# Dilated attention and a binary convolution on one core: from which chunk on the order of the instruction queues is written out by hand

## The chip, the core and the metric

The kernel runs on one core of one Trainium2 chip. The metric is device time in microseconds (us), the median of several executions; for the kernel before these were 5062.21, 5062.40 and 5062.62 us. A core has five engines, each with its own instruction queue that is worked off in order: TensorE (PE, matrix products), VectorE (DVE), ScalarE (ACT), GpSimd (POOL) and SyncE (SP, which here only issues DMAs). An instruction that waits for another engine holds up everything behind it in its own queue. So the order of the five queues, fixed when the program is built, is part of the kernel.

## The reference

Input `x` is 16 images of 56 x 56 pixels with 384 channels, float32. Two layers follow each other:

```python
# layer 0: dilated local attention, on the group-normalised input
x = x + _L0_conv_ref(_gn(x), L0_conv_w_qkv, L0_conv_w_proj, L0_conv_b_proj)
# layer 1: depthwise 3x3 convolution with weights clipped and reduced to their sign
x = x + _L1_conv_ref(_gn(x), L1_conv_w)

# in _L0_conv_ref: three channel groups with dilations 1, 2 and 3, four heads of 32 channels each
qkv = jnp.einsum('bchw,oc->bohw', xc, w_qkv)
attn = jnp.einsum('bgdn,bgdkn->bgnk', qg, ku) * scale     # 9 neighbours of each pixel
attn = jax.nn.softmax(attn, axis=-1)
out = jnp.einsum('bgnk,bgdkn->bgnd', attn, vu)
return jnp.einsum('bhwc,oc->bhwo', y, w_proj) + b_proj
```

`_gn` normalises over 32 groups of 12 channels, with mean and variance over a whole image. So nothing of an image can be normalised before all of it has been read.

## The kernel before

**Chunks and three plans.** An image is cut into 7 chunks of 8 rows (448 pixels), which makes 112 chunks. Three plans work on a chunk:

- `plan_a` (L453) reads it (`xin`, L469), turns pixels into columns on PE (`pt_x`, L474: three groups of four transposes), copies the result out of PSUM on ACT (L487), takes statistics on DVE (L489) and stores it in DRAM as `xd` (L492, L494). Of image 0 the turned chunks also stay on chip as `x_first`; chunks 10, 12 and 14 read into a second kind of buffer (`xin_z`), since `xin` has one buffer only.
- `plan_b` (L508) is the attention: load `xn` (L518), normalise (ACT, L522), project k and v (`pkv`, L526; copied to halo buffers by ACT, L539; halo rows passed between neighbouring chunks by small DMAs, L547 and L548), project q (`pq`, L526). DVE multiplies q by the shifted k (`t`, L591, nine instructions of three neighbours each), PE sums over a head's channels in three bursts of 8, 8 and 11 (`ps`, L572), then comes the softmax (L611 to L646; it ends with a DMA that writes `aT`). PE spreads the weights (`pb_a`, L658, nine times), DVE multiplies them by the shifted v (`w`, L669), POOL adds up (L679 to L683), PE applies the output projection (`po`, L696), DVE adds residual and bias (L701).
- `plan_c` (L733) is the convolution of the second layer. It starts ten chunks after `plan_b`, so it plays no part in the first ten chunks. The mean and scale that it needs in another layout go through a small DRAM tile (`mrd` and `mrz`, L404 to L412).

**Order by due times.** Every step is a "piece" with a due time. The table `WHEN` (L34 to L65) gives the due times of the steps of one chunk in units of which 9 (`STEP`, L949) make a chunk; `put` (L426) adds the chunk's start. Chunk m of `plan_b` starts at 9 m, its first steps are due at negative offsets. Everything that prepares the constants and reads image 0 is due before 0. At the end the pieces are traced in the order of their due times (L1007).

**Who decides the order of a queue.** Left alone, the framework's scheduler places instructions when the program is built: it goes by priority, which follows the order of tracing, but lets an instruction pass others that by its own reckoning cannot start yet. `pin` (L986) takes this freedom away: it gives each new instruction a dependence, without a semaphore, on the instruction traced before it on the same engine, so the queue is exactly the traced one. It does so for pieces whose due time lies between `FROM` and `UNTIL` (L952, L1008). Before the change this holds from due time 0 on, on all five engines.

**Bursts.** `in_one_go` (L335) keeps a group of matmuls together. In a pinned piece they simply follow each other; in a piece that is not pinned the first is placed like any other instruction, and the rest get high priority and keep their order.

Of the kernel before, what the change touches and what calls it, by code (L numbers as in the profile page):

```python
# [70 lines left out]
def dilated_attention_then_binary_conv(  # L71
# [33 lines left out]
    N = B * NCH  # L105
# [316 lines left out]
    def at(when, piece):  # L422

        pieces.setdefault(round(when, 4), []).append(piece)
# [524 lines left out]
    STEP = 9  # L949
    FIRST = -200  # L950
    FIXED = [getattr(mybir.EngineType, name) for name in FIXED_ENGINES]
    FROM, UNTIL = 0, STEP * N + 14  # L952
    at(FIRST + .14, load_weights)
    for cc in range(NG):
        at(FIRST + 6 + 2 * cc + .12, lambda cc=cc: turn_qkv_weights(cc))
# [84 lines left out]
```

## Time and profile before

| | |
|---|---|
| median of 3 runs | 5062.4 us |
| the profiled execution | 5064.99 us |
| its span, first to last instruction | 5063.3 us |
| PE busy | 4883.1 us, 96% of the span |
| DVE busy | 4455.8 us, 88% |
| POOL busy | 4224.4 us, 83% |
| ACT busy | 2524.2 us, 50% |
| granted PE clock, mean | 0.98 |
| chain that ended last | PE 86%, DVE 4%, DMA 4% |

The page divides the span into 40 slices and gives for each the tenths of it that an engine was busy; other views give the busy time of every engine in stretches that one chooses, and the instructions of a stretch in order of time. In these, a bracket at the end of a line gives how long the engine had been idle before it and what ended that. The clock granted to PE is given as a share of full speed.

### The profile page before, as it was taken

Reading aid. Unit: us, or ns where it says so; the run is one execution under the profiler, and the core shown is the slowest. Engines: PE = TensorE matmul, PEld = TensorE weight load, DVE = VectorE, ACT = ScalarE, POOL = GpSimd, SP = SyncE. Lnnn points to the kernel's source line nnn. Section 1 sums busy time; section 2 is a strip of 40 time slices with the busy share of each in tenths; the row PEclk is TensorE's granted clock in tenths of the full one; section 3 lists DMA queues with packets and bytes.
Section 4 is the critical chain, followed back from the end, with each engine's and each line's share of the span. In section 5 each row is a group of like instructions: output and inputs, shape, how many; then the busy total and the mean of one; then the engine's idle time right before and its main releaser. Section 6 shows DMA issues by size and latency. Waiting matters only on the chain.

```text
span 5063.3 us, 70210 instructions
## 1 busy us (share of the span) xinstructions
PE 4883.1 (96%) x24325; PEld 2249.2 (44%) x24325; DVE 4455.8 (88%) x4559; ACT 2524.2 (50%) x4501; POOL 4224.4 (83%) x2862
## 2 busy tenths in 40 slices
PE   7899999999999999999999999999999999999965
PEld 4444444444444444444444444444444444444422
DVE  4788999999999999999999999999999999888856
ACT  3122555555555555555555555555555555555445
POOL 2577889888898888889888888888889888898970
PEclk9999999999999999999999999999999999999976
DMA  5344666666666666666666666666666666655545
GB/s 155 108 126 118 176 176 172 174 169 176 168 183 172 170 173 170 176 175 182 165 178 176 177 177 176 180 173 172 178 163 182 176 169 174 156 147 141 141 135 153
DMA packets 831098, 836.43 MB, mean 165 GB/s; under 512 B 379796, under 2 KB 800023, under 8 KB 830743
## 3 DMA queue, kind: packets, MB, share of 16 engines
q1 hardware_dynamic: 822758, 819.95, 61.5%
q10 hardware_dynamic: 7984, 12.00, 0.7%
q8 instruction: 192, 3.15, 0.3%
q14 instruction: 164, 1.34, 0.1%
HBM read 477.52 MB, written 231.24 MB: 140 GB/s over the span
## 4 chain that ended last, share of the span: by engine, by line
PE 86%; DVE 4%; DMA 4%; POOL 2%; ACT 2%; SPq 2%; issue 1%; ACTq 0%; DVEq 0%; POOLq 0%
PE pkv L526 27%; PE pq L526 15%; PE po L696 14%; PE ps L572 11%; PE pc L817 6%; PE pb_a L658 5%; PE pt_x L474 3%; PE pt_o L908 3%; DVE t L591 2%; DMA xd<-xa 1%; DVE w L669 1%; PE pt_s L615 1%; ACT z L786 1%; POOL w L679 1%; DMA mrz<-mrd 0%
## 5 line engine op out<-in xcount | busy, mean ns | idle before, releaser
L679 POOL TENSOR_TENSOR w<-w 128x1344 f32<-128x1344 f32 x672 | 2054.6, 3057 | 275.3 <-DVE w L669 268.4
L669 DVE TENSOR_TENSOR w<-pb_a,v 128x1344 f32<-128x1344 f32 x1008 | 1561.4, 1549 | 231.6 <-PE pb_a L658 164.2
L591 DVE TENSOR_TENSOR t<-pq,k 128x1344 f32<-128x1344 f32 x1008 | 1542.2, 1549 | 100.6 <-PE pq L526 98.8
L526 PE MATMUL pkv<-xn,wqkvT 128*128 128x448 f32 x3924 | 1593.0, 547 | 0.0
L526 PEld LDWEIGHTS pkv<-xn,wqkvT 128*128 128x128 f32 x3924 | 718.5, 190 | 644.6 <-issue 623.2
L696 PE MATMUL po<-y,wprojT 128*128 128x448 f32 x2016 | 808.3, 546 | 8.8 <-POOL y L683 8.8
L526 PE MATMUL pq<-xn,wqkvT 128*128 128x448 f32 x1962 | 807.5, 548 | 7.9 <-DVE t L591 7.8
L572 PE MATMUL ps<-t,sel 128*32 128x448 f32 x6048 | 659.0, 545 | 9.4 <-DVE t L591 9.4
L891 POOL TENSOR_TENSOR m<-m 128x1344 f32<-128x1344 f32 x210 | 639.6, 3046 | 27.3 <-ACT m L881 19.1
L786 ACT ACTIVATE z<-z,mrz 96x448 f32<-96x448 f32 x840 | 570.3, 753 | 29.2 <-DMA mrz<-mrd 24.2
L881 ACT ACTIVATE m<-zg,ktap 128x448 f32<-128x448 f32 x945 | 540.7, 658 | 3.6 <-POOL m L891 3.6
L696 PEld LDWEIGHTS po<-y,wprojT 128*128 128x128 f32 x2016 | 378.5, 193 | 351.1 <-issue 320.3
L611 ACT COPY sT<-ps 128x448 f32<-128x448 f32 x112 | 59.8, 534 | 894.8 <-PE ps L572 894.8
L526 PEld LDWEIGHTS pq<-xn,wqkvT 128*128 128x128 f32 x1962 | 354.4, 190 | 312.7 <-issue 300.4
L539 ACT COPY k<-pkv 128x448 f32<-128x448 f32 x336 | 180.9, 538 | 575.4 <-PE pkv L526 574.9
L683 POOL TENSOR_TENSOR y<-y,w 128x448 f32<-128x448 f32 x336 | 382.7, 1139 | 26.3
L682 POOL TENSOR_TENSOR y<-w 128x448 f32<-128x448 f32 x336 | 382.4, 1138 | 26.3
L658 PE MATMUL pb_a<-aT,spread 24*128 24x448 bf16 x3024 | 368.9, 359 | 23.9 <-DVE w L669 22.6
L817 PE MATMUL pc<-z,kdiag 96*32 96x440 f32 x3360 | 360.6, 548 | 28.6 <-ACT z L749 18.8
L658 PEld LDWEIGHTS <-spread 24*128 24x128 bf16 x3024 | 99.8, 91 | 648.7 <-issue 567.1
L914 ACT COPY osb<-pt_o 112x384 f32<-112x384 f32 x420 | 199.1, 474 | 291.9 <-PE pt_o L908 284.3
L636 POOL TENSOR_TENSOR rest<-ew,e 112x512 f32<-112x512 f32 x112 | 129.9, 1159 | 240.1 <-ACT e L633 240.1
(136 smaller groups left out, 4817.6 us busy)
## 6 DMA issues: line engine op xcount, KB each, us to landing
z<-x1d SPq DMA_DIRECT2D x570, 224.0 KB, 4.3
xr<-xd SPq DMA_DIRECT2D x112, 672.0 KB, 4.9
x1d<-xr SPq DMA_DIRECT2D x112, 672.0 KB, 3.5
xn<-xd SPq DMA_DIRECT2D x109, 672.0 KB, 4.8
xin<-in_x_dram SPq DMA_DIRECT2D x105, 672.0 KB, 7.3
xd<-xa SPq DMA_DIRECT2D x315, 224.0 KB, 4.3
out_dram<-osb SPq DMA_DIRECT2D x420, 168.0 KB, 4.1
x<-x1d SPq DMA_DIRECT2D x80, 560.0 KB, 5.2
```

What stands on the lines that cost most here:

```text
L526: nc.tensor.matmul(dst[:, :PX], wqkvT[:, cc, o0 : o0 + P], had["xn"][:, cc, :], start=(cc == 0), stop=(cc == NG - 1))
L572: return nc.tensor.matmul(had["ps"][32 * j : 32 * j + 32, :PX], sel[:, s0 : s0 + 32], tk, start=(issued[j] == 1), stop=(issued[j] == len(r ...
L591: nc.vector.tensor_tensor(t.rearrange("p k (r w) -> p k r w", w=W), q3, k3, ALU.mult)
L658: return nc.tensor.matmul(pb[:, kx, :PX].rearrange("p (s n) -> p s n", s=NSUB), spread[rows_of, v % 2, :], had["a"][rows_of, :, v // 8, :] ...
L669: nc.vector.tensor_tensor(w.rearrange("p k (r w) -> p k r w", w=W), pb[:, :, :PX].rearrange("p k (r w) -> p k r w", w=W), three(kv[1][g][m ...
L679: nc.gpsimd.tensor_tensor(w0, w0, w, ALU.add)
L683: nc.gpsimd.tensor_tensor(y, y, w0[:, 2], ALU.add)
L696: nc.tensor.matmul(po[:, :PX], wprojT[:, g, j * P : (j + 1) * P], had[f"y{g}"], start=(g == 0), stop=(g == NG - 1))
L786: nc.scalar.activation(z, z, AF.Identity, bias=mrz[:, j, q, 0:1], scale=mrz[:, j, q, 1:2])
L817: return nc.tensor.matmul(pcr[q * HD : (q + 1) * HD, :, x0:x1], kdiag[:, kx // 2, j * NQ + q, :], rows(set_of(j, q))[:, :, x0 + kx - 1 : x ...
L881: nc.scalar.activation(rows(t[:, kx]), zp[:, ky : ky + ROWS, kx : kx + W], AF.Copy, scale=ktap[:, JG, o : o + 1])
L891: nc.gpsimd.tensor_tensor(had["m"], had["m"], t, ALU.add)
```

## The change

One line: the lower bound of the range in which pieces are pinned.

```diff
@@ -949,7 +949,7 @@
     STEP = 9
     FIRST = -200
     FIXED = [getattr(mybir.EngineType, name) for name in FIXED_ENGINES]
-    FROM, UNTIL = 0, STEP * N + 14
+    FROM, UNTIL = 9 * STEP, STEP * N + 14
     at(FIRST + .14, load_weights)
```

Pieces due from 0 up to 81, which are those of the first nine chunks, are no longer pinned; they join those due before 0, which were not pinned either. From 81 on nothing changes: the first pinned instruction of each engine hangs on the last one traced before it. No instruction is added or removed, no buffer changes its size. The passage of mean and scale through DRAM is in both kernels and untouched.

Instructions per engine and where the two built programs differ in order:

| engine | instructions | first place that differs | last place that differs |
|---|---|---|---|
| PE | 18287 | 151 | 1132 |
| DVE | 4561 | 8 | 301 |
| ACT | 4542 | 46 | 185 |
| POOL | 2867 | 93 | 262 |
| SP | 3461 | 21 | 172 |

The last differing PE place falls at about 390 us in the trace of the kernel before.

## The prediction

> **What bounds the kernel now.** I read the page's slices first, then the busy time in stretches of 100 us.
>
> ```profile
> PE   7899999999999999999999999999999999999965
> PEclk9999999999999999999999999999999999999976
> ...
> 0.00:100.00 100.00, 65.48 (x289) 43.14 (x292) 36.39 (x67) 29.51 (x55) 24.89 (x136) 0.92 0.56 159
> 100.00:200.00 100.00, 84.08 (x374) 38.67 (x368) 71.42 (x68) 22.39 (x43) 42.26 (x23) 0.94 0.42 117
> 200.00:300.00 100.00, 97.66 (x434) 45.09 (x433) 85.58 (x88) 22.00 (x41) 72.34 (x56) 0.98 0.42 119
> 900.00:1000.00 100.00, 100.00 (x495) 46.92 (x489) 92.30 (x93) 49.97 (x89) 89.23 (x60) 1.00 0.61 155
> ```
>
> The third number of a stretch is PE's busy time, the clock stands third from the end. From 500 us on PE has hardly a gap: what is gained before that moves the whole rest forward, and nothing else can gain. The change reorders only up to about 390 us. So the question is how much PE time is lost there, and how much of it the new order wins back.
>
> PE's instructions in order of time, those with idle time ahead of them:
>
> ```profile
> 65.05 2.52 PE L526 MATMUL pkv<-x_first,wqkvT 128*128 128x448 f32 x6 [1.13 <-ACT x_first L522]
> 68.06 0.57 PE L474 MATMUL pt_x<-ident,xin 112*128 112x112 f32 x4 [0.49 <-DMA xin<-in_x_dram]
> 77.83 2.49 PE L526 MATMUL pq<-x_first,wqkvT 128*128 128x448 f32 x6 [1.65 <-DVE t L591]
> 97.59 4.15 PE L572 MATMUL ps<-t,sel 128*32 128x448 f32 x22 [4.58 <-DVE t L591]
> 112.34 0.57 PE L474 MATMUL pt_x<-ident,xin_z 112*128 112x112 f32 x4 [2.74 <-DMA xin_z<-in_x_dram]
> 128.71 1.71 PE L572 MATMUL ps<-t,sel 128*32 128x448 f32 x16 [0.36 <-DVE t L591]
> 137.75 3.81 PE L572 MATMUL ps<-t,sel 128*32 128x448 f32 x22 [4.28 <-DVE t L591]
> 154.38 0.57 PE L474 MATMUL pt_x<-ident,xin_z 112*128 112x112 f32 x4 [3.74 <-DMA xin_z<-in_x_dram]
> 198.28 0.98 PE L474 MATMUL pt_x<-ident,xin_z 112*128 112x112 f32 x4 [3.89 <-DMA xin_z<-in_x_dram]
> ```
>
> With four more between 168 and 222 us (0.81, 0.23, 0.81, 0.15) that is 24.9 us of idle time between 60 and 240 us. From 240 to 390 us only 0.86 us per chunk of 39.6 us are left (0.30 before a `pb_a`, 0.56 elsewhere). Two causes stand out: the first transposes of chunks 10, 12 and 14 wait for their load, and the third score burst waits for the last products `t`.
>
> A gap costs more than its length. The clock around the gap that ends at 97.59:
>
> ```profile
> 94.00:96.00 2.00, 0.00 (x0) 0.00 (x0) 2.00 (x3) 0.00 (x0) 0.00 (x0) 1.00 0.00 0
> 96.00:98.00 2.00, 0.41 (x4) 0.17 (x8) 1.54 (x2) 0.00 (x0) 0.00 (x0) 0.94 0.00 0
> 98.00:100.00 2.00, 2.00 (x16) 0.64 (x11) 0.00 (x0) 0.00 (x0) 0.00 (x0) 0.50 0.00 0
> 100.00:102.00 2.00, 2.00 (x11) 0.50 (x5) 0.00 (x0) 0.18 (x1) 0.00 (x0) 0.71 0.00 0
> 102.00:104.00 2.00, 2.00 (x6) 0.90 (x5) 0.00 (x0) 0.35 (x1) 0.00 (x0) 1.00 0.00 0
> ```
>
> Half clock from 97.7 to 101.2 us, 3.4 us long. The burst of 22 rows took 4.15 us; at the 1.71 us of 16 rows it would be 2.35, so 1.8 us are lost. In such stretches half clock also stands at 138.7 (3.4 us), 155.8 (3.4) and 196.7 (6.8, of which PE worked 5.3). Lost: 1.7 + 1.7 + 1.7 + 2.6 = 7.7 us. [...] In all 24.9 + 7.7 = 32.6 us are lost between 60 and 240 us.
>
> [...] gaps of 3.74 to 4.58 us brought half clock, in multiples of 3.41 us, the one of 2.74 us did not. [...]
>
> ```profile
> 83.74 0.54 SPq L469 DMA_DIRECT2D xin<-in_x_dram  x1
> 105.23 0.34 SPq L492 DMA_DIRECT2D xd<-xa  x1
> ...
> 106.84 0.58 SPq L469 DMA_DIRECT2D xin_z<-in_x_dram  x1
> ```
>
> For 21 us SP issued nothing: a store stood waiting for its copy on ACT, with the load of chunk 10 three places behind. Issued at 106.84, it let PE start at 112.34.
>
> **The change part by part.** I compared the built orders and gave each instruction its duration from this trace; times below are on the clock of before.
>
> *Loads of chunks 10, 12 and 14.* In the new SP queue the loads into `xin_z` for 10 and 12 stand before every store of `xa` and every halo copy; each waits only for the transposes of image 0 that free its buffer (done by 36 and 40 us). That of chunk 14 stands ahead of the halo copies of v of its turn and long after chunk 10's transposes. So all three land tens of us early. The gain is 2.74 + 3.74 + 3.89 = 10.4 us of idle time and 1.7 + 2.6 = 4.3 us of clock: 14.7 us.
>
> *Third burst of chunk 0.* Before, PE goes from `pq` straight to the burst of 11 and waits for three `t` (4.49 us). Now three `pkv` (2.4 us) and four transposes (0.57 us) stand between. 4.58 - 3.0 leaves 1.6; I take 1.8[...]. Gain 2.8 + 1.7 = 4.5 us. In chunk 1 three `pkv`, four transposes and two `pb_a` stand there; with DVE's `w` between the `t` I find 2.0 us left in two pieces: 2.3 + 1.7 = 4.0 us.
>
> *First chunks.* ACT now normalises chunks 0 and 1 in one go while PE is still on the first k, so the 1.13 us at 65.05 go; `pkv` for chunk 1 now stands before the second `pq`, so the 1.65 us at 77.83 go; of the 0.49 at 68.06 (a load issued at the same moment as before) 0.2 go. Together 3.0 us. The rest (0.36 + 0.81 + 1.19 = 2.4 us) I leave.
>
> Sum: 14.7 + 4.5 + 4.0 + 3.0 = 26.2 us.
>
> *What it costs at the front.* DVE prepares the small weights (L291 to L319) before the last seven statistics of image 0, where it used to do so from 64 us on; they wait for the nine small loads of L258. The last of these was issued at 29.94 and its kind lands in a median of 4.5 us: 34.4. Twenty instructions take 3.5 us (64.26 to 67.73 before), to 37.9; seven statistics of 0.63 to 42.3, an aggregate 0.34, two statistics 1.26, two aggregates 0.53: 44.4, where before the last ended at 43.55. All that PE can do next hangs on it: 0.9 us lost. If a small load lands at its slowest 10.8 us it would be up to 7 us, my outer bound[...].
>
> *Softmax on POOL.* In the new order the second `w` sum of a pair goes ahead of the softmax remainder, and two `y` sums of 1.14 us stand among its parts. A steady chunk before:
>
> ```profile
> 325.56 1.16 POOL L636 TENSOR_TENSOR rest<-ew,e 112x512 f32<-112x512 f32 x1 [6.32 <-ACT e L633]
> 328.66 2.92 SPq L644 DMA_TRANSPOSE aT<-e  x1
> 336.61 0.37 PE L658 MATMUL pb_a<-aT,spread 24*128 24x448 bf16 x3
> ```
>
> The `w` sum (3.06 us) fits into the 6.32 us that POOL stood idle. The two `y` put `aT` off by 2.3 us. It lands 4.1 us after its issue, at 332.8; the first `pb_a` of the chunk came at 336.61, so 3.8 us are to spare. Hidden by 1.5 us; without that cover each us of delay is a us of PE per chunk.
>
> *Waits not foreseen.* Going through a steady chunk in the new order, I found PE waiting nowhere over 0.1 us, with DVE 4 us short of full. The first chunks are less regular. Bounds: -4 us (the 0.86 us of four steady chunks vanish) to +12 (2 us in each of six). I take +3.
>
> Net: 26.2 - 0.9 - 3 = 22.3, so 22 us. On the profiled execution: span 5063.3 - 22 = 5041.3, with the 1.7 us around it 5043. The profiled run is 2.6 us above the median of the runs, so the median becomes 5062.4 - 22 = 5040.4.
>
> **The rivals.**
>
> *The waits only move.* PE ahead of its feeders finds DVE or ACT late instead: the 14.7 us of the loads are won, but the bursts lose as much elsewhere and the front costs 2 to 7 us. Net 3 to 13 us, middle 8: 5054. For it: DVE is 82% busy at 180 to 200 us (16.35 of 20), and ACT now has three normalisations of `xn` ahead of the copy of the scores. Against: a DVE 71% busy between 100 and 200 us has room.
>
> *Slower: `aT` comes too late in every chunk.* If the remainder on POOL waits not for two `y` but for a backlog of `w`, `aT` is late by 5 us beyond its cover in the seven chunks 2 to 8. [...] 7 x 6.7 = 47 us against 25 won, 5084. It decides from 3.6 us per chunk on (7 x 3.6 = 25). Against: POOL is 72% busy there and was idle just before the remainder.
>
> *It does nothing.* The built orders differ in some 900 places on PE alone; excluded.
>
> **How the numbers follow.** Forecast 0.70 (gains of 14 to 32 us), waits only move 0.20 (0.08 of it still over 0.2%), slower 0.10 (0.08 by over 0.2%). A measurement of this kernel tells about 0.2%, 10 us, from no change. Faster 0.70 + 0.08 = 0.78; same 0.12 + 0.02 = 0.14; slower 0.08. The range: the forecast's best, 32 us, gives 5030; upwards it takes in most of the second case, 5056. Left out are the slower case and a little of the rest, some 0.15.
>
> **What would show it.** Right: no wait of PE for `xin_z` below 250 us; full clock from about 60 us on; no gap over 3.4 us; the first `pb_a` near 115 us instead of 122.98; PE over 93 us busy between 100 and 200 us. The first normalisation on ACT, 52.64 before, at about 53.5 (front cost). Wrong: PE waiting for `aT` or `w` in every chunk from 200 to 390 us, half clock in the slices after the first, or gaps that open after 390 us in the part whose order is unchanged.

## The result, and the profile after

| | before | changed |
|---|---|---|
| median | 5062.0 us (6 runs) | 5044.4 us (6 runs) |
| profiled execution | 5064.99 us | 5046.37 us |
| its span | 5063.3 us | 5044.6 us |

The ratio is 0.9967, with a 95% interval of 0.9957 to 0.9977: 17.6 us faster by the medians, where 22 were forecast. That is a third of a percent, and clear of the noise. On a second chip, beside the experiments below, the same kernel again gave 0.9967 (0.9956 to 0.9978).

The page of the changed kernel, the same two rows as before:

```profile
PE   7999999999999999999999999999999999999965
PEclk8999999999999999999999999999999999999975
```

And its busy time in stretches of 100 us (PE busy is the third number, the clock stands third from the end):

```profile
100.00:200.00 100.00, 96.08 (x448) 43.83 (x447) 87.61 (x85) 26.43 (x49) 58.81 (x33) 1.00 0.46 126
200.00:300.00 100.00, 94.01 (x420) 42.01 (x413) 79.66 (x79) 19.33 (x34) 67.47 (x56) 0.97 0.34 101
300.00:400.00 100.00, 98.49 (x427) 44.14 (x427) 89.72 (x86) 21.70 (x40) 70.53 (x43) 1.00 0.38 106
```

Between 100 and 200 us PE works 96.1 us instead of 84.1, as hoped. Between 200 and 300 us it works 94.0 where it worked 97.7 before: something was lost there that the prediction did not have. PE's waits in the changed kernel, in order of time, show what:

```profile
69.35 0.57 PE L474 MATMUL pt_x<-ident,xin 112*128 112x112 f32 x4 [0.67 <-DMA xin<-in_x_dram]
95.63 4.15 PE L572 MATMUL ps<-t,sel 128*32 128x448 f32 x22 [1.94 <-DVE t L591]
130.01 2.46 PE L572 MATMUL ps<-t,sel 128*32 128x448 f32 x22 [1.44 <-DVE t L591]
145.48 2.52 PE L526 MATMUL pq<-x_first,wqkvT 128*128 128x448 f32 x6 [0.18 <-DVE t L591]
155.57 0.37 PE L658 MATMUL pb_a<-aT,spread 24*128 24x448 bf16 x3 [1.88 <-DVE w L669]
198.72 1.71 PE L572 MATMUL ps<-t,sel 128*32 128x448 f32 x16 [0.41 <-DVE t L591]
219.89 0.35 PE L377 MATMUL pv<-dev,gsel 128*32 128x1 f32 x6 [1.06 <-POOL dev L372]
229.37 1.43 PE L397 MATMUL pp<-pair,gselT 32*128 32x2 f32 x6 [4.67 <-POOL pair L392]
```

The waits for `xin_z` are gone and the two long waits before the third bursts are 1.9 and 1.4 us. New are two waits for POOL in the statistics of image 1 (`group_norm`, L345), the second followed by half clock from 229.18 to 236.01 us:

```profile
229.18:236.01 6.83, 6.64 (x16) 4.04 (x16) 3.63 (x4) 0.39 (x1) 0.28 (x2) 0.50 0.59 160
```

The lead of the changed kernel, as the start of the first `pb_a` of a chunk before less that after, in the two profiled executions:

| first `pb_a` of chunk | 0 | 1 | 2 | 3 | 4 | 5 | 6 | 7 |
|---|---|---|---|---|---|---|---|---|
| before, us | 123.0 | 168.5 | 216.0 | 257.5 | 297.0 | 336.6 | 376.2 | 415.8 |
| lead, us | 7.5 | 12.9 | 23.1 | 13.0 | 13.8 | 14.6 | 15.4 | 16.0 |

23 us are won by chunk 2, 10 are lost before chunk 3, 0.8 us a chunk come back. From there on the lead keeps between 15.8 and 18.9 us.

Why POOL was late, in its own order of time:

```profile
221.57 0.18 POOL L388 TENSOR_TENSOR var<-var 32x1 f32<-32x1 f32 x1 [1.73 <-DVE var L385]
...
222.89 0.18 POOL L389 TENSOR_TENSOR var<-var 32x1 f32<-32x1 f32 x1
223.04 1.15 POOL L636 TENSOR_TENSOR rest<-ew,e 112x512 f32<-112x512 f32 x1
224.17 0.18 POOL L390 TENSOR_SCALAR var<-var 32x1 f32<-32x1 f32 x1
224.43 0.18 POOL L391 TENSOR_TENSOR var<-var 32x1 f32<-32x1 f32 x1
224.56 0.60 POOL L640 CAST e<-rest 112x512 bf16<-112x512 f32 x1
225.14 0.18 POOL L388 TENSOR_TENSOR var<-var 32x1 f32<-32x1 f32 x1
225.28 1.12 POOL L682 TENSOR_TENSOR y<-w 128x448 f32<-128x448 f32 x1
...
229.13 0.18 POOL L392 TENSOR_TENSOR pair<-pair 32x1 f32<-32x1 f32 x1
```

The thirteen small operations of L388 to L392 each use the result of the one before. In the free order, sums of `y` and parts of the softmax stand between them. The thirteen took 7.74 us (221.57 to 229.31); in the kernel before they stood together and took 3.36 us (241.61 to 244.97), from first to last:

```profile
241.61 0.18 POOL L388 TENSOR_TENSOR var<-var 32x1 f32<-32x1 f32 x1 [1.67 <-DVE var L385]
...
244.79 0.18 POOL L392 TENSOR_TENSOR pair<-pair 32x1 f32<-32x1 f32 x1
```

### The profile page after: what moved, and what is told of

Read it like the earlier page. It is cut to its first block, busy times and chain, and to the rows that moved or that the text cites. A ratio compares the mean times of both kernels' runs of the same rounds, so it can differ in the third digit from the quotient of the medians.

```text
span 5044.6 us, 70251 instructions
## 1 busy us (share of the span) xinstructions
PE 4881.7 (97%) x24325; PEld 2246.1 (45%) x24325; DVE 4453.8 (88%) x4559; ACT 2525.3 (50%) x4501; POOL 4223.8 (84%) x2862
## 4 chain that ended last, share of the span: by engine, by line
PE 82%; DMA 3%; DVE 3%; POOL 2%; ACT 1%; SPq 1%; issue 1%; ACTq 0%; DVEq 0%; POOLq 0%
PE pkv L526 26%; PE pq L526 14%; PE po L696 13%; PE ps L572 11%; PE pc L817 7%; PE pb_a L658 5%; PE pt_o L908 3%; PE pt_x L474 2%; DMA xd<-xa 1%; DVE t L591 1%; PE pt_s L615 1%; ACT z L786 1%; DVE w L669 1%; POOL w L679 1%; DMA mrz<-mrd 0%
## 5 line engine op out<-in xcount | busy, mean ns | idle before, releaser
L682 POOL TENSOR_TENSOR y<-w 128x448 f32<-128x448 f32 x336 | 382.3, 1138 | 25.7
L658 PE MATMUL pb_a<-aT,spread 24*128 24x448 bf16 x3024 | 368.9, 359 | 22.8 <-DVE w L669 22.4
L572 PEld LDWEIGHTS ps<-t,sel 128*32 128x32 f32 x6048 | 179.7, 109 | 322.1 <-issue 293.9
```

What stands on the lines that cost most here:

```text
L572: return nc.tensor.matmul(had["ps"][32 * j : 32 * j + 32, :PX], sel[:, s0 : s0 + 32], tk, start=(issued[j] == 1), stop=(issued[j] == len(r ...
L658: return nc.tensor.matmul(pb[:, kx, :PX].rearrange("p (s n) -> p s n", s=NSUB), spread[rows_of, v % 2, :], had["a"][rows_of, :, v // 8, :] ...
```

## Experiments

Each run was timed in five rounds beside the kernel before on the same chip; the two groups were on a second chip, where the kernel before took 5055.3 us (25 runs) and 5055.4 us (26 runs). The only trace of before is from the first chip, so all leads are counted against that one. The changed kernel itself has leads of 26.9, 18.4 and 21.4 us at chunks 2, 3 and 7 on the second chip, 3.7 to 5.4 us more than on the first. So a lead of a run on the second chip is read against these numbers, or against the same trace's lead at another chunk. By their intervals the gains in time are good to 3 to 7 us.

### Is the loss at 220 to 236 us the fault of the order, or does a lead have to fall back there?

**Pinned from chunk 4 on.** The statistics of image 1 are due from 38.5 to 47.

```diff
-    FROM, UNTIL = 9 * STEP, STEP * N + 14
+    FROM, UNTIL = 4 * STEP, STEP * N + 14
```

> Pinned from due time 36 on (chunk 4) instead of 81, so that the statistics of image 1 (due 38.5 to 47) are in the written order again. Theory 1 (the new order won about 23 us by 193 us, and lost 9 of them because the statistics of image 1 were torn apart on POOL): no PE wait for POOL before pp near 230 us, no half clock there, first pb_a of chunk 3 about 22 us ahead of the kernel before, time 8 us under the changed kernel, about 5036. Theory 2 (PE had simply run ahead of what DVE and POOL can feed, so the lead has to fall back at that point whatever the order): a lead of 13 to 16 us again at 260 us, time within 2 us of the changed kernel, 5044.

Measured: 5032.8 us, ratio 0.9952 (0.9940 to 0.9965), 22.4 us under the kernel before and 5.4 under the changed kernel on that chip, where 8 were expected. No wait of PE for POOL stands in its trace between 51 us and the end phase, and no half clock between 55 us and the end phase. The lead is 24.9 us at chunk 2 and still 24.9 at chunk 7. The 0.30 and 0.56 us per chunk of the written order are back:

```profile
263.86 0.36 PE L658 MATMUL pb_a<-aT,spread 24*128 24x448 bf16 x3 [0.30 <-DVE w L669]
265.33 2.52 PE L526 MATMUL pq<-xn,wqkvT 128*128 128x448 f32 x6 [0.56 <-DVE t L591]
```

A lead need not fall back; theory 2 falls by the trace, since the times of the two kernels overlap in their intervals.

**POOL alone in the written order for the small operations.**

```diff
-            pin(FIXED if newest["pinned"] else ())
+            pin(FIXED if newest["pinned"] else FIXED[3:4] if 44.6 <= when < 45.6 else ())
```

> The changed kernel, with POOL alone pinned for the pieces due from 44.6 to 45.6: the thirteen small operations of the statistics of image 1 stand together again ahead of the softmax remainder, all else stays free. Theory 1: the thirteen take 3.4 us instead of 7.7, the 4.67 us wait before pp falls to under 1.5, no half clock at 229 us (another 3.4), so 6 to 8 us under the changed kernel, about 5037. Theory 2 (the lead falls back whatever the order): within 2 us of the changed kernel.

Measured: 5034.4 us, ratio 0.9955 (0.9941 to 0.9968), 20.9 us under the kernel before, against 17.2 for the changed kernel on that chip. POOL and PE in its trace:

```profile
217.64 0.18 POOL L388 TENSOR_TENSOR var<-var 32x1 f32<-32x1 f32 x1 [2.70 <-DVE var L385]
...
220.81 0.18 POOL L392 TENSOR_TENSOR pair<-pair 32x1 f32<-32x1 f32 x1
```

```profile
221.05 0.83 PE L397 MATMUL pp<-pair,gselT 32*128 32x2 f32 x6 [0.28 <-POOL pair L392]
234.93 0.36 PE L658 MATMUL pb_a<-aT,spread 24*128 24x448 bf16 x3 [1.98 <-DMA aT<-e]
```

The thirteen take 3.35 us, the wait before `pp` falls from 4.67 to 0.28 us, and there is no half clock. Part is given back: the softmax that now stands behind them and between two sums of `w` has its `aT` late, and PE waits 1.98 us for it. From chunk 2 to chunk 3 the lead falls by 3.4 us, where it falls by 8.5 in the changed kernel on that chip. So the traces show the small operations on POOL as the cause of the long wait and of the half clock behind it. In time the gain is nearer 4 us than the 6 to 8 expected, and single runs of the two kernels mix (5027.8 to 5035.8 us against 5033.6 to 5045.8), so the time by itself does not show it.

**Free, pinned at the statistics, free again.**

```diff
-        newest["pinned"] = FROM <= when < UNTIL
+        newest["pinned"] = 4 * STEP <= when < 48 or FROM <= when < UNTIL
```

> The changed kernel, with everything pinned once more for due times 36 to 48 alone, where the statistics of image 1 are worked out; free again from 48 to 81. Theory 1: the loss at the statistics goes (6 to 9 us), and the waits of 0.3 and 0.56 us per chunk that the written order has in chunks 5 to 8 stay away as they do in the changed kernel, 0.8 us per chunk: 2 to 3 us better than pinned from 36 on, so 24 to 27 us under the kernel before. Theory 2 (a lead has to fall back at that point): as the changed kernel.

Measured: 5031.9 us, ratio 0.9952 (0.9938 to 0.9965), 23.5 us under the kernel before, where 24 to 27 were expected. The lead is 24.3 us at chunk 3 and 26.5 at chunk 7. The loss is gone and the 2 us of the steady chunks show in the trace; in the times the two are not to be told apart (0.9952 both).

### What carries the 23 us: the early loads or PE's order?

**Only SP's queue free** (from the kernel before; the other four built orders are identical to it).

```diff
-            pin(FIXED if newest["pinned"] else ())
+            pin(() if not newest["pinned"] else FIXED[:4] if when < 9 * STEP else FIXED)
```

> The kernel before, with SP's queue alone left free below due time 81; the four other queues are exactly as before. Theory 1 (loads won 14.7 us by themselves): no PE wait for xin_z, the waits of 4.58 and 4.28 us before the third bursts stay with their half clock, time 14 to 15 us under the kernel before, about 5048. Rival (the gain is that of PE's order, and early loads only move the wait to the next operand): under 6 us, above 5056.

Measured: 5050.9 us, ratio 0.9988 (0.9982 to 0.9995; 21 runs): 4.4 us. PE's waits:

```profile
98.13 3.82 PE L572 MATMUL ps<-t,sel 128*32 128x448 f32 x22 [4.58 <-DVE t L591]
115.42 2.52 PE L526 MATMUL pq<-x_first,wqkvT 128*128 128x448 f32 x6 [2.19 <-DVE t L591]
...
137.47 4.63 PE L572 MATMUL ps<-t,sel 128*32 128x448 f32 x22 [4.28 <-DVE t L591]
156.31 0.37 PE L658 MATMUL pb_a<-aT,spread 24*128 24x448 bf16 x3 [2.19 <-DVE w L669]
157.77 2.52 PE L526 MATMUL pq<-x_first,wqkvT 128*128 128x448 f32 x6 [0.57 <-DVE t L591]
```

No wait for `xin_z` is left, but at each of the three places PE now runs a few us further and waits for DVE: 2.19; 2.19 and 0.57; and 0.57 and 0.56 near 199 us. Of 10.4 us of idle time, 6.1 have only moved. The 4.3 that are left are close to the 4.4 measured, but this sum leaves the clock out: from 60 to 240 us half clock stands for 10.2 us here and for 17.1 before, and the lead in this trace is 7.6 us from chunk 2 on. The traced run, 5047.4 us, was 3.5 us under the median. The forecast of theory 1, 14 to 15 us for the loads by themselves, is refuted; the rival's "under 6 us" came out.

**All but SP's queue free** (from the changed kernel).

```diff
-            pin(FIXED if newest["pinned"] else ())
+            pin(FIXED if newest["pinned"] else FIXED[4:] if when >= 0 else ())
```

> The changed kernel, with SP's queue pinned from due time 0 as in the kernel before; the other four queues are free below 81. Theory 1: the waits for xin_z are back (10.4 us and half clock, 14.7 together), the bursts and first chunks keep their 11.5 us, the statistics still lose 9: about 3 us under the kernel before, 5057 to 5062. Rival (PE's order carries the gain): 10 us or more under the kernel before.

This edit also pins SP after `UNTIL`, which was not meant; from the start of the last output projection to the end its trace takes 150.3 us, and the ten traces lie between 149.5 and 153.8, so nothing shows of it. Measured: 5041.8 us, ratio 0.9968 (0.9955 to 0.9980), 13.4 us under the kernel before. Only one wait for `xin_z` came back (3.33 us at 179 us). SP issues the three loads at 93.65, 129.76 and 173.72 us instead of 106.84, 148.86 and 192.65: the store ahead of the first waits for its copy on ACT, which now starts at 91.48 us instead of 104.67. Free orders elsewhere bring that copy forward; PE's alone brings it to 97.85, in a trace shown below, and which of the others does the rest was not taken apart. Theory 1's 5057 to 5062 is refuted; the rival's "10 us or more" came out.

**Only PE's queue free, and PE's and SP's.**

```diff
-            pin(FIXED if newest["pinned"] else ())
+            pin(FIXED if newest["pinned"] else FIXED[1:] if 0 <= when < FROM else ())
```

> The kernel before with PE's queue alone left free below due time 81; DVE, ACT, POOL and SP are exactly as before. Theory 3 (what counts is that PE has something to do while it waits; early loads only shift a wait): 10 to 18 us under the kernel before, more than the loads alone won, first pb_a of chunk 1 over 8 us ahead, and no loss at the statistics of image 1, since POOL is in the written order. Theory 1 (loads 14.7, bursts and first chunks 11.5, separately): 7 to 11 us, and the waits for xin_z of 2.7 to 3.9 us stay.

For the second, `FIXED[1:4]` takes the place of `FIXED[1:]`, with this expected:

> PE's and SP's queues free below due time 81; DVE, ACT and POOL exactly as before. Theory 3: 2 to 5 us better than PE alone, at or above the changed kernel's gain, 16 to 22 us under the kernel before. Theory 1: the sum of 14.7 and 7 to 11, so 22 to 26 us. If the orders of DVE and ACT were needed for the gain: no better than PE alone.

Measured: PE alone 5044.8 us, ratio 0.9981 (0.9974 to 0.9987; 21 runs), 10.6 us; PE and SP 5029.7 us, 0.9950 (0.9937 to 0.9962), 25.7 us. PE's waits with PE alone free, first, and with both, second (the waits from 52 us to 430 us that are over 2 us, and in the second the one before them):

```profile
105.31 0.98 PE L474 MATMUL pt_x<-ident,xin_z 112*128 112x112 f32 x4 [3.24 <-DMA xin_z<-in_x_dram]
134.29 3.63 PE L572 MATMUL ps<-t,sel 128*32 128x448 f32 x22 [2.20 <-DVE t L591]
149.22 0.98 PE L474 MATMUL pt_x<-ident,xin_z 112*128 112x112 f32 x4 [4.65 <-DMA xin_z<-in_x_dram]
192.49 0.57 PE L474 MATMUL pt_x<-ident,xin_z 112*128 112x112 f32 x4 [3.79 <-DMA xin_z<-in_x_dram]
```

```profile
94.36 2.46 PE L572 MATMUL ps<-t,sel 128*32 128x448 f32 x22 [1.94 <-DVE t L591]
127.96 2.46 PE L572 MATMUL ps<-t,sel 128*32 128x448 f32 x22 [2.19 <-DVE t L591]
```

With PE alone the long waits before the bursts shrink to 1.94 and 2.20 us, and the loads are waited for as long as ever. With both, the sum is more than its parts: 25.7 us against 4.4 + 10.6 = 15.0. So the worth of the early loads depends on what stands beside them: 4.4 us alone, 25.7 - 10.6 = 15.1 on top of PE's free order, and 17.2 - 13.4 = 3.8 on top of the other four free orders, where two of the three loads are in time anyway. The free orders of DVE, ACT and POOL were not needed for the gain: with those three in the written order, the statistics on POOL stay whole and the lead holds (25.9 us at chunk 2, 25.7 at chunk 3). Neither theory came out whole. Of theory 3, the 10.6 us for PE alone lie at the edge of its 10 to 18, but the first `pb_a` of chunk 1 is 4.4 us ahead in place of over 8, SP's share is 15.1 us in place of 2 to 5, and the two together are above its 16 to 22. Of theory 1, the 7 to 11 us for PE alone and the 22 to 26 for both came out, and only the loads alone failed.

**The changed kernel once more** beside them:

> The changed kernel itself, once more, on the same chip as the three others of this group, so that differences of a few us between them can be read. Both theories: 15 to 19 us under the kernel before.

Measured: 5038.2 us, 17.2 us under the kernel before, as expected, with 4.66 us before `pp`; half clock follows it for 3.41 us here.

Four versions beat the changed kernel by their medians: PE and SP free (25.7 us), the island (23.5), pinned from chunk 4 (22.4), POOL set right (20.9). Their intervals overlap each other and that of the changed kernel. Run by run, all five of PE and SP free (5027.4 to 5030.8 us) and all five of the island (5028.5 to 5033.3) lie under all six of the changed kernel beside them (5033.6 to 5045.8).

## Why the prediction was right, and where it was not

The direction, the place and the range held. The size, 22 us against 17.6, is off mainly by one term, "waits not foreseen": put at 3 us, it came to about 7, 10 lost before chunk 3 and 3 won back after it. Of its signs of being right two failed with it: a gap of 4.67 us opened, and half clock came twice between 60 and 240 us (3.41 us from 96.06 us on, 6.83 us from 229.18 us on).

*What bounds the kernel.* Right: all that was won before 390 us was kept by a PE that is busy almost without a gap. Lost clock time after the gaps of 3.74 to 4.58 us was a real part of the gain: half clock stood for 17.1 us between 60 and 240 us before, and for 10.2 us in the changed kernel.

*Third bursts and first chunks (4.5 + 4.0 + 3.0 us).* The gaps left are 1.94 and 1.44 us where 1.8 and 2.0 were worked out. The first `pb_a` came at 115.5 us where "near 115" stood. That agreement is partly luck: in that trace half clock did follow the gap of 1.94 us, for 3.41 us, against the forecast, and on the second chip, where it did not, the same kernel came to its first `pb_a` at 111.7. That gaps of 1.8 and 2.0 us would keep full clock, 1.7 us in each burst, was an estimate of mine; the trace of before has one gap of 2.74 us that kept it, and none of that length. The last section takes this up.

*Loads (14.7 us).* The waits went as said, and on top of PE's free order the loads were worth 15.1 us. What did not hold is that they stand as a term of their own: "The gain is 2.74 + 3.74 + 3.89" takes the whole wait as gain without asking what PE meets next. With the loads alone that is DVE, 1 to 3 us on, and the runs gave 4.4 us; with the other four orders free, they added 3.8. The sum for all parts together, 26.2 less 0.9, is close to the lead by chunk 2, 23.1 us on the first chip and 26.9 on the second. So the sum was right, and its division among the parts depends on the order in which they are freed. Why the parts help each other is read from the traces, and no run takes it apart further.

*Front (0.9 us).* The number came out by another way. The small loads were in time. The last aggregate ended at 43.92 instead of 43.55, 0.4 us later, and the first normalisation on ACT came at 52.74, 0.1 us later than before, where "about 53.5" was forecast. The first transposes after it did come 0.9 us later (58.71, before 57.80), but because half clock lasted until 58.52 us instead of 56.78, and the first `pkv` took 4.46 us instead of 3.65. On the second chip the same kernel had its half clock end at 55.52 and these transposes at 56.62, so this 0.9 us was luck.

*Softmax on POOL.* Hidden, as said: PE waits nowhere for `aT` in the changed kernel.

*Waits not foreseen (+3 us).* The term that was mis-sized. The steady chunks gave back 0.8 us each, 3 us by chunk 7, its lower bound nearly; but "going through a steady chunk" left out the one piece that comes once in seven chunks. The statistics of image 1 cost 1.06 + 4.67 us of idle time, and half clock while PE worked 6.6 us, another 3.3: 9 us, of the 10 that the lead lost. The built order of POOL had shown the small operations apart; I read it only for the softmax.

*The rivals.* "The waits only move" is what happens when SP alone is freed: 4.4 us. The slower case, `aT` late in every chunk, shows nowhere; its 6.7 us per chunk were 5 us of waiting and an estimate of 1.7 us of clock, half of the 3.41 us of half clock that followed each of the gaps of 4.58 and 4.28 us in the trace of before. One wait of 1.98 us for `aT` stands in the run with POOL set right.

## What to carry to other kernels

When a wait is removed from an engine with an ordered queue, price the next operand behind it before booking the wait as gain; a load made early and a reordered queue of the engine that waits for it can be worth more together than the sum of each (25.7 us against 15.0 here). A chain of tiny dependent operations grows by whatever a scheduler puts between them (3.36 us became 7.74 here), so where another engine waits for its end, pin it as a block. A free order is best judged engine by engine: here freeing PE and SP gave the gain, and what the free order of POOL put between the small operations took some of it back.

## What the runs showed of the hardware that was not expected

The gap of 2.74 us in the trace of before had kept full clock, and I took shorter gaps for safe. The same gap of 1.94 us before the third burst of chunk 0 stands in eight traces. In two of them the burst of 22 rows behind it took 4.15 us (the changed kernel on the first chip) and 4.10 us (all but SP's queue free), in the other six 2.46 us. The changed kernel on the first chip, where half clock stood from 96.06 to 99.48 us:

```profile
94.00:96.00 2.00, 0.37 (x4) 0.17 (x8) 2.00 (x3) 1.13 (x3) 0.00 (x0) 1.00 0.64 217
96.00:98.00 2.00, 2.00 (x16) 0.59 (x11) 0.10 (x1) 1.24 (x2) 0.00 (x0) 0.52 0.17 62
```

The same kernel on the second chip:

```profile
94.00:96.00 2.00, 2.00 (x23) 0.53 (x15) 0.04 (x1) 1.32 (x3) 0.00 (x0) 1.00 0.13 48
96.00:98.00 2.00, 2.00 (x12) 1.20 (x10) 0.56 (x1) 0.53 (x1) 0.00 (x0) 1.00 0.00 0
```

Before the third burst of chunk 1 it is much the same: behind 2.20 us of idle time the burst took 3.63 us with PE alone free, behind 2.19 us it took 2.46 us with PE and SP free. And in the changed kernel on the first chip a gap of 1.88 us, ending at 155.57 us, left the clock at 1.00. So in these traces the length of a gap did not by itself tell whether half clock followed; what decided it was not shown, and no run was made to find out. The 1.7 us lost before 100 us (4.15 us in place of 2.46) are one reason why single traces of the same kernel differ by a few us.

The kernel before itself spread from 5049.0 to 5063.4 us in 26 runs on the second chip, and from 5059.3 to 5062.6 in 6 runs on the first.
